# Summing the outputs of a bias network's second layer: one more addition by DMA, and half the third-layer matmuls

## The chip, the cores and the metric

The kernel runs on one core of a Trainium2 chip. The metric is the device time of one execution in microseconds (us). PE is the matmul engine, DVE the vector engine, ACT the scalar engine, POOL the GpSimd engine and SP the engine that issues most transfers. POOL issues the transfers that add to their destination, SP the plain ones.

## The reference

Four layers follow one another on a tensor of 2 x 512 x 32 x 32. The change is in the first, an attention whose keys are sampled at learned places. Cut to what matters (G = 8 groups, 64 keys, 1024 queries, two images):

```python
pos  = grid_q[:, :, None, :] - grid_kv[:, None, :, :]      # 16 x 1024 x 64 x 2
bias = sign(pos) * log1p(abs(pos))
bias = relu(bias @ cpb_w1 + cpb_b1)                        # 2 -> 128
bias = relu(bias @ cpb_w2 + cpb_b2)                        # 128 -> 128
bias = (bias @ cpb_w3 + cpb_b3).reshape(b, G, 1024, 64)    # 128 -> 1
sim  = einsum('bhid,bhjd->bhij', qh, kh) + bias
out  = einsum('bhij,bhjd->bhid', softmax(sim), vh)
x    = x + conv1x1(out)                                    # then an MLP, and three more layers
```

The bias network runs for each of 16 (image, group) and each of 64 keys on 1024 queries: a million positions with 128 features each. It takes most of the kernel's time.

## The kernel before

All is float32. `g` counts 8 steps: four chunks of 128 channels (two heads each) by two images. Within a step there are J = 64 keys; `n` counts all 512 keys, `p` their 256 pairs.

**First layer** (`first`, L351, DVE). The position feature of x depends on the column alone and that of y on the row alone, so the first layer is a table of columns plus a table of rows, with the relu folded into the same instruction. For one key it writes `h1`, 128 features x 2048 positions (32 rows, 2 heads, 32 columns). Four buffers of `h1` are all the lead that DVE can have over PE.

**Second layer** (`second`, L617, PE). The 128 outputs are taken in four sets `o` of 32. For a pair of keys and a set there are 8 matmuls of 32 outputs x 512 positions: four blocks of positions, each to its own 32 partitions of `ph`, for two keys. ACT applies bias and relu (L626) and leaves `r0` to `r3` in turn, each 128 partitions (4 blocks x 32 outputs) x 2 keys x 512. The weights have been scaled by the size of the third layer's weights, so what is left of the third layer is a sum with signs. The outputs were sorted at the start (`counted`, with the constants `same`, `below`, `place`, `rank`): among those that will be added to one another, sets 0 and 2 hold only the sign of the majority, and `rel` (plus or minus one) carries that of sets 1 and 3.

**Summing.** `combine` (L632, DVE) adds r1 to r0 and r3 to r2, with `rel`. `join` (L635, POOL's DMA) adds r2 to r0. Each block now has 32 sums per position and key. `shift` (L642, two DMAs of SP) copies, for the first key of the pair, one half of the partitions of r0 to the other half of a tile `xs`, and for the second key the reverse; `fold` (L647, two DMAs of POOL) adds the remaining partitions. One `xs` tile (128 x 512) thus holds one pair, 16 sums of each key.

**Third layer** (`third`, L656, PE). For 8 keys (four pairs), four matmuls of 32 rows, one per pair and each to its own 32 partitions of `psim`, sum each key's 16 partitions with their sign (`cw3`). Four such calls fill one `psim` tile of 32 keys: 8 calls for a step g, 64 in all.

**The order.** The engines' orders are fixed by the program: `pin` keeps them. The loop over pairs issues the second layer, and between sets runs what `at(n, when, ...)` has registered for key n. Registered are the attention of the step before (`attend`), the sampling and projection of the next step's keys and values (`prepare`, with `keys` on ACT, L725, and `values` on DVE, L737), the offset network of the later chunks (`Chain`, whose 36 taps, L229, run on DVE among the tables of keys 4 to 84 and 95 to 211), the table loads of SP and their scaling on ACT (L172), and the summing:

```python
for u in range(8):
    at(J * g + 8 * u + 14, 0, third, g, u)
...
at(2 * p + 4, 0, shift, p)
at(2 * p + 5, 0, fold, p)
```

`join` of a pair is issued during the next pair. The tile `co` holds the sample coordinates of all chunks. After the loop, `po` (L1035) applies the output weights to the attention's result; the scheduler mixes its matmuls with the last third-layer sets and the last step's softmax.

Of the kernel before, what the change touches and what calls it, by code (L numbers as in the profile page):

```python
# [10 lines left out]
F32 = mybir.dt.float32  # L11
AF = mybir.ActivationFunctionType
ALU = mybir.AluOpType
# [3 lines left out]
P = 128  # L17
B, C, H, W = 2, 512, 32, 32
HW = H * W
NT = B * HW  # L20
KC = C // P
TK = 8
DH = 64
J = 64
# [3 lines left out]
MID = C // 4  # L28
SE = C // 16
EPS = 1e-5  # L30
FMAX = float(np.finfo(np.float32).max)


# [21 lines left out]

_CONSTS = [("ident", P), ("grid", 2 * J), ("gridf", J), ("npx", 1), ("npy", 8), ("sel3", 2)]

_ORDER = [("same", P), ("below", P), ("place", P), ("rank", 1), ("third", 35)]
_CAT, _n = {}, 0
for _name, _w in _CONSTS:  # L60
    _CAT[_name] = (_n, _w)
# [10 lines left out]
def conv_seq(  # L72
# [20 lines left out]
    nc = tc.nc  # L93
# [6 lines left out]
    x = keep.tile([P, KC, NT], F32, name="x")  # L100
# [33 lines left out]
    with ExitStack() as ctx_l0:  # L134
        l0 = ctx_l0.enter_context(tc.tile_pool(name="l0", bufs=1))
# [2 lines left out]
        kblk = l0.tile([P, 2, 2, J], F32, name="kblk")  # L138
        vblk = l0.tile([P, 2, 2, J], F32, name="vblk")

        co = l0.tile([P, 2, 2, KC * B * J], F32, name="co")
        kvw = l0.tile([P, 2, KC, P], F32, name="kvw")
        wo = l0.tile([P, KC, C], F32, name="wo")
        ctx_att = ctx_l0.enter_context(ExitStack())
# [41 lines left out]
        def pin(ins):  # L186
            return tc.keep_in_program_order(ins) if started else ins
# [12 lines left out]
        class Chain:  # L200


            def __init__(self, k0, k1, alloc):
                self.k0, self.n, self.alloc = k0, (k1 - k0) * P, alloc
                self.g = slice(k0 * B, k1 * B)
                self.cs = slice(k0 * P, k1 * P)
                self.sums = {}

            def tile(self, name):
# [123 lines left out]

        w2a = l0.tile([P, 4, 32], F32, name="w2a")
        sb3 = l0.tile([P, 4, 2], F32, name="sb3")
        cw3 = l0.tile([P, 35], F32, name="cw3")
        rel = l0.tile([P, 2], F32, name="rel")

        h1p = ctx_att.enter_context(tc.tile_pool(name="h1p", bufs=4))
# [21 lines left out]
        with tc.tile_pool(name="a", bufs=1) as a, tc.tile_pool(name="aps", bufs=3, space=PSUM) as aps, tc.tile_pool(  # L363
            name="apc", bufs=1, space=PSUM
# [95 lines left out]
            def counted():  # L460
                pin(ve.tensor_copy(od[:, 7:9], pcnt))
                pin(ve.tensor_scalar(cpbw, cpbw, maj, None, ALU.mult))


                pin(ve.tensor_scalar(maj, total, 4.0, None, ALU.is_ge))
                pin(ve.tensor_scalar(t0, maj, -1.0, 1.0, ALU.mult, ALU.add))
                pin(ve.tensor_scalar(t1, total, -1.0, 8.0, ALU.mult, ALU.add))
# [127 lines left out]
        with tc.tile_pool(name="hid", bufs=3) as hid, tc.tile_pool(name="sm", bufs=1) as sm, tc.tile_pool(name="hps", bufs=2, space=PSUM) as hps, tc.tile_pool(  # L595
# [1 line left out]
        ) as sps, tc.tile_pool(name="mps", bufs=2, space=PSUM) as mps:  # L597
            NG, NK = KC * B, KC * B * J
            rs, psims = {}, {}
            todo = {}  # L600

            def at(n, when, fn, *args):

                todo.setdefault((n, when), []).append((fn, args))
# [5 lines left out]
            def second(p, o):  # L610

                ph = hps.tile([P, 2, 512], F32, name="ph")
                for i in range(2):
                    for t in range(4):
                        half, h = divmod(t, 2)
                        pin(
                            nc.tensor.matmul(  # L617
                                ph[t * 32 : (t + 1) * 32, i, :],
                                lhsT=w2a[:, o],
                                rhs=h1s[2 * p + i][:, half * 16 : (half + 1) * 16, h, :],  # L620
                                start=True,
                                stop=True,
                            )
                        )
                r = hid.tile([P, 2, 512], F32, name=f"r{o}", bufs=(4, 1, 3, 1)[o])
                pin(nc.scalar.activation(r, ph, AF.Relu, bias=sb3[:, o, 1:2]))  # L626
                rs[p, o] = r

# [5 lines left out]
            def join(p):  # L634
                pin(nc.gpsimd.dma_start(rs[p, 0], rs.pop((p, 2)), accum_op=ALU.add))  # L635

            def shift(p):

                r = rs[p, 0]
                xs = rs[p] = hid.tile([P, 512], F32, name="xs", bufs=5)  # L640
                for i in range(2):
                    pin(nc.sync.dma_start(xs[i::2], r[1 - i :: 2, i, :]))  # L642

            def fold(p):
                r = rs.pop((p, 0))
                for i in range(2):
                    pin(nc.gpsimd.dma_start(rs[p][i::2], r[i::2, i, :], accum_op=ALU.add))  # L647

            def third(g, u):
                kb, i = divmod(u, 4)  # L650
                p = (g * J + 8 * u) // 2
                if i == 0:
                    psims[g, kb] = sps.tile([P, 512], F32, name=f"psim{kb}")
                for m in range(4):
                    pin(
                        nc.tensor.matmul(  # L656
                            psims[g, kb][m * 32 : (m + 1) * 32, :],
                            lhsT=cw3[:, 3 - i : 35 - i],
                            rhs=rs.pop(p + m),
                            start=(i == 0),  # L660
                            stop=(i == 3),
                            skip_group_check=True,
                        )
                    )

            def prepare(g):

                k, b = divmod(g, B)
                st = {}
                n = J * (g - 1) + 30  # L670
                def hat(t):
                    if t == 0:
                        st["smp"] = smpp.tile([P, 8, 2, J], F32, name="smp")
                    pin(
                        nc.scalar.activation(
                            st["smp"][:, t],
                            co[:, 1, :, g * J : (g + 1) * J],
                            AF.Abs,
                            bias=c("npy")[:, t : t + 1],
                        )  # L680
                    )
# [4 lines left out]

                def cross(i):
                    sp = st["smp"][:, 4 * i : 4 * i + 4]
                    hx = co[:, 0, :, g * J : (g + 1) * J]
# [21 lines left out]
                def project():  # L711
                    st["pk"] = mps.tile([P, 2, J], F32, name="pk", tag="m")
                    for i in range(2):
# [3 lines left out]
                            )  # L717
                        )

                def keys():  # L720

                    for h in range(2):
                        hs = slice(h * DH, (h + 1) * DH)
                        pin(
                            nc.scalar.activation(  # L725
                                kblk[hs, g % 2, h, :].rearrange("p (k x i) -> p k x i", k=2, i=4),
                                st["pk"][hs, 0, :].rearrange("p (k i x) -> p k x i", k=2, i=4),
                                AF.Identity,
                                scale=DH**-0.5,
                            )  # L730
                        )

                def values():
                    for h in range(2):
                        hs = slice(h * DH, (h + 1) * DH)
                        pin(
                            nc.vector.tensor_copy(  # L737
                                vblk[hs, g % 2, h, :].rearrange("p (k x i) -> p k x i", k=2, i=4),
                                st["pk"][hs, 1, :].rearrange("p (k i x) -> p k x i", k=2, i=4),
                            )  # L740
                        )

                def weigh():
                    pw = st["pw"] = mps.tile([P, C], F32, name="pw", tag="m")
# [152 lines left out]
                    )  # L897
            for g in range(NG):
                prepare(g)
                for u in range(8):  # L900
                    at(J * g + 8 * u + 14, 0, third, g, u)
                if g < NG - 1:
                    attend(g, J * (g + 1) + 7, True)
            for p in range(NK // 2):
                at(2 * p + 4, 0, shift, p)
                at(2 * p + 5, 0, fold, p)

            def chain(k0, k1, n, taken):
                ch = Chain(k0, k1, lambda shape, name: mps.tile(shape, F32, name=name, tag="m"))
# [11 lines left out]
                for dn, when, fn, *args in plan:  # L921
                    at(n + dn, when, fn, *args)

            chain(1, 2, 84, 80)
            chain(2, 4, 211, 116)


            for k in range(KC):
# [951 lines left out]
def _layout(a):  # L1880
# [34 lines left out]
    def put(name, x, to=consts):  # L1915
        at, w = _CAT[name]
        to[:, at : at + w] = x
# [17 lines left out]
    put("place", np.array([0, 1, 4, 5, 2, 3, 6, 7])[rank].astype(f)[None], order)  # L1935
    put("rank", rank.astype(f)[:, None], order)
    put("third", (np.arange(35)[None] == (3 + 8 * (p // 32) + 4 * (p % 2))[:, None]).astype(f), order)
    put("npy", -(4 * np.arange(8)[None] + p[:, None] // 32).astype(f))


# [54 lines left out]
```

## Time and profile before

| | us |
|---|---|
| median of three runs | 2724.9 (2724.87 to 2726.49) |
| the profiled execution, its own time | 2726.49 |
| its span | 2724.7 |
| PE busy | 2681.3 |
| DVE busy | 2253.8 |
| ACT busy | 1538.4 |
| POOL busy | 670.2 |

A row of a group gives line, engine, operation, output <- inputs, shape and count; then busy time and mean ns of one; then the idle time of the engine just before these instructions and what ended most of it. One float32 matmul leaves two records. Matmuls on different column blocks run beside one another, so a row's mean of one is not its share of the time; the time from one set's start to the next one's is. The issues of DMAs give a median time from issue to landing: 4.8 us for `join` (512 KB), 4.7 for each DMA of `fold` and 2.2 for each of `shift` (128 KB each).

### The profile page before, as it was taken

Reading aid. Unit: us, or ns where it says so; the run is one execution under the profiler, and the core shown is the slowest. Engines: PE = TensorE matmul, PEld = TensorE weight load, DVE = VectorE, ACT = ScalarE, POOL = GpSimd, SP = SyncE. Lnnn points to the kernel's source line nnn. Section 1 sums busy time; section 2 is a strip of 40 time slices with the busy share of each in tenths; the row PEclk is TensorE's granted clock in tenths of the full one; section 3 lists DMA queues with packets and bytes.
Section 4 is the critical chain, followed back from the end, with each engine's and each line's share of the span. In section 5 each row is a group of like instructions: output and inputs, shape, how many; then the busy total and the mean of one; then the engine's idle time right before and its main releaser. Section 6 shows DMA issues by size and latency. Waiting matters only on the chain.

```text
span 2724.7 us, 49360 instructions
## 1 busy us (share of the span) xinstructions
PE 2681.3 (98%) x19830; PEld 978.1 (36%) x19830; DVE 2253.8 (83%) x1993; ACT 1538.4 (56%) x1904; POOL 670.2 (25%) x784
## 2 busy tenths in 40 slices
PE   8999999999999999999999999999999999999997
PEld 4223323232332323333333233333344444455544
DVE  6999999999999999999999999999554544615646
ACT  7676687667668766866766776776221111001334
POOL 0333333333333333333333333333100000000001
PEclk9999999999999999999999999999999999999998
DMA  3777777877777787777787788787410000100001
GB/s 128 165 167 164 161 157 156 172 154 161 168 155 160 155 174 155 161 167 157 168 193 164 157 174 189 156 172 157 94 30 23 16 23 24 39 38 1 0 0 62
DMA packets 146196, 335.13 MB, mean 123 GB/s; under 512 B 22672, under 2 KB 32400, under 8 KB 145200
## 3 DMA queue, kind: packets, MB, share of 16 engines
q0 software_dynamic: 77824, 201.38, 41.5%
q1 hardware_dynamic: 67568, 130.08, 13.6%
q8 instruction: 157, 2.57, 0.4%
q14 instruction: 71, 0.58, 0.1%
q10 hardware_dynamic: 576, 0.51, 0.1%
HBM read 58.99 MB, written 4.46 MB: 23 GB/s over the span
## 4 chain that ended last, share of the span: by engine, by line
PE 89%; DVE 6%; issue 3%; ACT 2%; DMA 0%; DVEq 0%; POOL 0%; ACTq 0%; POOLq 0%
PE ph L617 58%; PE A L1100 4%; PE D L1100 4%; PE C L1100 4%; PE B L1100 2%; PE psim L656 2%; PE po L1035 2%; DVE h L351 2%; DVE r L632 2%; PE pg L1243 1%; PE pa L1354 1%; PE pu L1277 1%; PE pscore L1486 1%; PE pz L1515 1%; PE pt L1506 1%
## 5 line engine op out<-in xcount | busy, mean ns | idle before, releaser
L617 PE MATMUL ph<-h,w2a 128*32 128x512 f32 x16384 | 1781.7, 592 | 4.3 <-ACT r L626 3.6
L626 ACT ACTIVATE r<-ph,sb 128x1024 f32<-128x1024 f32 x1024 | 1141.6, 1115 | 533.2 <-PE ph L617 508.1
L351 DVE CUSTOM_DVE_ANT_1 h<-tab 128x2048 f32<-128x2048 f32 x512 | 1171.1, 2287 | 22.4 <-PE ph L617 17.7
L617 PEld LDWEIGHTS ph<-h,w2a 128*32 128x32 f32 x16384 | 522.2, 109 | 1219.8 <-issue 832.0
L632 DVE SCALAR_TENSOR_TENSOR r<-r,rel,r 128x1024 f32<-128x1024 f32 x512 | 656.2, 1282 | 26.8 <-ACT r L626 26.5
L647 POOL DMA_DIRECT2D xs<-r x512 | 475.0, 1128 | 225.7 <-DMA xs<-r 122.7
L635 POOL DMA_DIRECT2D r<-r x256 | 222.6, 869 | 1047.8 <-DVE r L632 874.5
L172 ACT ACTIVATE tab<-tab,vec 128x256 f32<-128x256 f32 x252 | 137.1, 544 | 0.0
L1288 POOL MEMSET M<- 128x512 f32 x2 | 1.0, 518 | 443.8 <-DVE x L1164 443.8
L1140 ACT COPY u<-A 128x512 f32<-128x512 f32 x16 | 9.4, 586 | 146.9 <-PE A L1100 146.9
L1771 POOL TENSOR_TENSOR x<-x,aff 128x512 f32<-128x512 f32 x7 | 7.0, 1029 | 329.1 <-ACT e L1736 329.1
L1119 ACT ACTIVATE h<-h,vec 128x512 f32<-128x512 f32 x32 | 23.1, 721 | 113.6 <-DVE h L1122 113.6
L656 PE MATMUL psim<-xs,cw 128*32 128x512 f32 x512 | 70.5, 594 | 2.2 <-DMA xs<-r 2.2
L1122 DVE TENSOR_TENSOR h<-C,u 128x512 f32<-128x512 f32 x32 | 22.1, 691 | 47.7 <-PE C L1100 47.4
L1100 PE MATMUL A<-xn,w 128*128 128x512 f32 x128 | 60.3, 593 | 0.8 <-DVE x L1042 0.8
L1100 PE MATMUL C<-hT,w 128*128 128x512 f32 x128 | 60.3, 592 | 0.0
L1100 PE MATMUL A<-h,w 128*128 128x512 f32 x128 | 60.1, 592 | 0.0
L1035 PE MATMUL po<-q,vwo 128*128 128x512 f32 x128 | 57.1, 599 | 0.0
L229 DVE SCALAR_TENSOR_TENSOR acc<-q,vec,acc 128x128 f32<-128x128 f32 (+3 forms) x88 | 45.9, 521 | 0.8
L1160 DVE TENSOR_TENSOR x<-D,x 128x512 f32<-128x512 f32 x32 | 22.1, 691 | 26.0 <-PE D L1100 26.0
L852 ACT ACTIVATE e<-e,den 128x64 f32<-128x64 f32 x128 | 41.8, 337 | 2.2 <-DVE den L848 2.2
L1160 DVE TENSOR_TENSOR x<-C,x 128x512 f32<-128x512 f32 x32 | 22.1, 691 | 24.8 <-PE C L1100 24.8
(364 smaller groups left out, 1840.3 us busy)
## 6 DMA issues: line engine op xcount, KB each, us to landing
r<-r POOLq DMA_DIRECT2D x256, 512.0 KB, 4.8
xs<-r SPq DMA_DIRECT2D x512, 128.0 KB, 2.2
xs<-r POOLq DMA_DIRECT2D x512, 128.0 KB, 4.7
tab<-fd SPq DMA_DIRECT2D x63, 512.0 KB, 6.2
lw<-in_l_w_dram SPq DMA_DIRECT2D x5, 1024.0 KB, 9.1
x<-in_x_dram SPq DMA_DIRECT2D x4, 1024.0 KB, 9.0
w<-in_mlp_w_dram SPq DMA_DIRECT2D x8, 512.0 KB, 4.4
w<-in_mlp_w_dram SPq DMA_DIRECT2D x16, 256.0 KB, 3.2
```

Source lines behind the costliest of these rows:

```text
L172: return nc.scalar.activation(tf, tf if src is None else src[:, :, ax, :], AF.Identity, bias=0.0 if ax == 0 else v("L0_conv_cpb_b1"), scal ...
L229: pin(nc.vector.scalar_tensor_tensor(dst, src, wt_, dst, ALU.mult, ALU.add))
L351: nc.vector._custom_dve(TENSOR_ADD_SAT, out=h1, in0=columns.unsqueeze(1).to_broadcast([P, 32, 2, 32]), in1=rows_.unsqueeze(3).to_broadcast ...
L617: nc.tensor.matmul(ph[t * 32 : (t + 1) * 32, i, :], lhsT=w2a[:, o], rhs=h1s[2 * p + i][:, half * 16 : (half + 1) * 16, h, :], start=True, ...
L626: pin(nc.scalar.activation(r, ph, AF.Relu, bias=sb3[:, o, 1:2]))
L632: pin(nc.vector.scalar_tensor_tensor(r0, r1, rel[:, i : i + 1], r0, ALU.mult, ALU.add))
L635: pin(nc.gpsimd.dma_start(rs[p, 0], rs.pop((p, 2)), accum_op=ALU.add))
L647: pin(nc.gpsimd.dma_start(rs[p][i::2], r[i::2, i, :], accum_op=ALU.add))
L656: nc.tensor.matmul(psims[g, kb][m * 32 : (m + 1) * 32, :], lhsT=cw3[:, 3 - i : 35 - i], rhs=rs.pop(p + m), start=(i == 0), stop=(i == 3), ...
L1035: nc.tensor.matmul(po, lhsT=vwo[:, k * B + t // 2, o * P : (o + 1) * P], rhs=q[:, k, ts_], start=(k == 0), stop=(k == KC - 1),)
L1100: nc.tensor.matmul(banks[bank], lhsT=a[an][k], rhs=b_[bn_][k], start=(i < 4 and k == 0), stop=(k == n - 1), skip_group_check=True,)
L1160: nc.vector.tensor_tensor(to, t, to, ALU.add)
```

## The change

For one pair, the summing goes one step further before the third layer. `fold` now adds in place, in r0 itself, every odd partition to the even one before it, both keys in one DMA. `shift` copies every fourth partition of r0 to partitions d, d+4, ... of `xs`, and `meet` adds to them the partitions two further on. An `xs` tile (now 128 x 2 x 512, three buffers instead of five of half the size) takes d = 0 to 3, four pairs; each key has 8 sums. The third layer runs on two `xs` tiles at a time, 16 keys in four matmuls: four calls for a step g, 32 in all. The order of outputs at the start is over sets of 16 instead of 8, `r0` has five buffers instead of four, `co` keeps three chunks instead of four (the third chunk takes the first one's place), and `keys` and `values` write their new key order in four small copies each instead of two. The dates in the list move to fit.

```diff
+CO_AT = (1, 0, 1, 2)
...
-        co = l0.tile([P, 2, 2, KC * B * J], F32, name="co")
+        co = l0.tile([P, 2, 2, 3 * B * J], F32, name="co")
...
-                pin(ve.tensor_scalar(maj, total, 4.0, None, ALU.is_ge))
+                pin(ve.tensor_scalar(maj, total, 8.0, None, ALU.is_ge))
...
-                r = hid.tile([P, 2, 512], F32, name=f"r{o}", bufs=(4, 1, 3, 1)[o])
+                r = hid.tile([P, 2, 512], F32, name=f"r{o}", bufs=(5, 1, 3, 1)[o])
...
+            def fold(p):
+                r = rs[p, 0]
+                pin(nc.gpsimd.dma_start(r[0::2], r[1::2], accum_op=ALU.add))
+
             def shift(p):
-                r = rs[p, 0]
-                xs = rs[p] = hid.tile([P, 512], F32, name="xs", bufs=5)
-                for i in range(2):
-                    pin(nc.sync.dma_start(xs[i::2], r[1 - i :: 2, i, :]))
-
-            def fold(p):
-                r = rs.pop((p, 0))
-                for i in range(2):
-                    pin(nc.gpsimd.dma_start(rs[p][i::2], r[i::2, i, :], accum_op=ALU.add))
+                t, d = divmod(p, 4)
+                if d == 0:
+                    xs_[t] = hid.tile([P, 2, 512], F32, name="xs", bufs=3)
+                pin(nc.sync.dma_start(xs_[t][d::4], rs[p, 0][0::4]))
+
+            def meet(p):
+                t, d = divmod(p, 4)
+                pin(nc.gpsimd.dma_start(xs_[t][d::4], rs.pop((p, 0))[2::4], accum_op=ALU.add))
 
             def third(g, u):
-                kb, i = divmod(u, 4)
-                p = (g * J + 8 * u) // 2
+                kb, i = divmod(u, 2)
                 if i == 0:
                     psims[g, kb] = sps.tile([P, 512], F32, name=f"psim{kb}")
-                for m in range(4):
-                    pin(
-                        nc.tensor.matmul(
-                            psims[g, kb][m * 32 : (m + 1) * 32, :],
-                            lhsT=cw3[:, 3 - i : 35 - i],
-                            rhs=rs.pop(p + m),
-                            start=(i == 0),
-                            stop=(i == 3),
-                            skip_group_check=True,
+                for a in range(2):
+                    xs = xs_.pop(g * J // 8 + 2 * u + a)
+                    for c in range(2):
+                        m = 2 * c + a
+                        pin(
+                            nc.tensor.matmul(
+                                psims[g, kb][m * 32 : (m + 1) * 32, :],
+                                lhsT=cw3[:, 1 - i : 33 - i],
+                                rhs=xs[:, c, :],
+                                start=(i == 0),
+                                stop=(i == 1),
+                                skip_group_check=True,
+                            )
                         )
-                    )
...
-                    for h in range(2):
-                        hs = slice(h * DH, (h + 1) * DH)
...
+                    for h, kb in np.ndindex(2, 2):
+                        hs, ks = slice(h * DH, (h + 1) * DH), slice(kb * 32, (kb + 1) * 32)
+                        to, of = ordered(kblk[hs, g % 2, h, ks], st["pk"][hs, 0, ks])
+                        pin(nc.scalar.activation(to, of, AF.Identity, scale=DH**-0.5))
...
-                for u in range(8):
-                    at(J * g + 8 * u + 14, 0, third, g, u)
+                for u in range(4):
+                    at(J * g + 16 * u + 24, 0, third, g, u)
                 if g < NG - 1:
-                    attend(g, J * (g + 1) + 7, True)
+                    attend(g, J * (g + 1) + 9, True)
             for p in range(NK // 2):
-                at(2 * p + 4, 0, shift, p)
-                at(2 * p + 5, 0, fold, p)
+                at(2 * p + 4, 0, fold, p)
+                at(2 * p + 6, 0, shift, p)
+                at(2 * p + 7, 0, meet, p)
...
-            chain(1, 2, 84, 80)
-            chain(2, 4, 211, 116)
+            chain(1, 2, 86, 82)
+            chain(2, 4, 213, 116)
...
-    rank = p // 32 * 2 + p % 2
-    same = p[:, None] % 32 // 2 == p[None] % 32 // 2
+    rank = p // 32 * 4 + p % 4
+    same = p[:, None] % 32 // 4 == p[None] % 32 // 4
```

More of the change, by code (lines that the diff above doesn't have):

```diff
@@ L56 @@
 _CONSTS = [("ident", P), ("grid", 2 * J), ("gridf", J), ("npx", 1), ("npy", 8), ("sel3", 2)]
-_ORDER = [("same", P), ("below", P), ("place", P), ("rank", 1), ("third", 35)]
+_ORDER = [("same", P), ("below", P), ("place", P), ("rank", 1), ("third", 33)]
 _CAT, _n = {}, 0
@@ L205, in __init__ @@
                 self.g = slice(k0 * B, k1 * B)
-                self.cs = slice(k0 * P, k1 * P)
+                self.cs = slice(CO_AT[k0] * P, (CO_AT[k0] + k1 - k0) * P)
                 self.sums = {}
@@ L337, in conv_seq @@
         sb3 = l0.tile([P, 4, 2], F32, name="sb3")
-        cw3 = l0.tile([P, 35], F32, name="cw3")
+        cw3 = l0.tile([P, 33], F32, name="cw3")
         rel = l0.tile([P, 2], F32, name="rel")
@@ L462, in counted @@
                 pin(ve.tensor_scalar(cpbw, cpbw, maj, None, ALU.mult))
-                pin(ve.tensor_scalar(maj, total, 4.0, None, ALU.is_ge))
+                pin(ve.tensor_scalar(maj, total, 8.0, None, ALU.is_ge))
                 pin(ve.tensor_scalar(t0, maj, -1.0, 1.0, ALU.mult, ALU.add))
-                pin(ve.tensor_scalar(t1, total, -1.0, 8.0, ALU.mult, ALU.add))
+                pin(ve.tensor_scalar(t1, total, -1.0, 16.0, ALU.mult, ALU.add))
                 pin(ve.scalar_tensor_tensor(t0, t1, t0, below, ALU.mult, ALU.add))
@@ L599, in conv_seq @@
             rs, psims = {}, {}
-            todo = {}
+            xs_, todo = {}, {}
             def at(n, when, fn, *args):
@@ L669, in prepare @@
                 st = {}
-                n = J * (g - 1) + 30
+                n = J * (g - 1) + 32
+                here = slice(CO_AT[k] * P + b * J, CO_AT[k] * P + (b + 1) * J)
                 def hat(t):
@@ L676, in hat @@
                             st["smp"][:, t],
-                            co[:, 1, :, g * J : (g + 1) * J],
+                            co[:, 1, :, here],
                             AF.Abs,
@@ L688, in cross @@
                     sp = st["smp"][:, 4 * i : 4 * i + 4]
-                    hx = co[:, 0, :, g * J : (g + 1) * J]
+                    hx = co[:, 0, :, here]
                     pin(nc.vector.tensor_tensor(sp, sp, hx.unsqueeze(1).to_broadcast([P, 4, 2, J]), ALU.mult))
@@ L718, in project, with ordered @@
                         )
+                def ordered(to, of):
+                    to, of = to.rearrange("p (c x i) -> p c x i", c=2, i=2), of.rearrange("p (i x c) -> p c x i", c=2, i=2)
+                    return to, of
                 def keys():
-                    for h in range(2):
-                        hs = slice(h * DH, (h + 1) * DH)
[L724 to L731, printed above, removed]
-                def values():
[L734 to L741, printed above, removed]
+                    for h, kb in np.ndindex(2, 2):
+                        hs, ks = slice(h * DH, (h + 1) * DH), slice(kb * 32, (kb + 1) * 32)
+                        to, of = ordered(kblk[hs, g % 2, h, ks], st["pk"][hs, 0, ks])
+                        pin(nc.scalar.activation(to, of, AF.Identity, scale=DH**-0.5))
+                def values():
+                    for h, kb in np.ndindex(2, 2):
+                        hs, ks = slice(h * DH, (h + 1) * DH), slice(kb * 32, (kb + 1) * 32)
+                        to, of = ordered(vblk[hs, g % 2, h, ks], st["pk"][hs, 1, ks])
+                        pin(nc.vector.tensor_copy(to, of))
                 def weigh():
@@ L1929, in _layout @@
     put("sel3", (p[:, None] % 32 == np.array([1, 2])[None]).astype(f))
-    rank = p // 32 * 2 + p % 2
-    same = p[:, None] % 32 // 2 == p[None] % 32 // 2
+    rank = p // 32 * 4 + p % 4
+    same = p[:, None] % 32 // 4 == p[None] % 32 // 4
     put("same", same.astype(f), order)
     put("below", (same & (rank[:, None] < rank[None])).astype(f), order)
-    put("place", np.array([0, 1, 4, 5, 2, 3, 6, 7])[rank].astype(f)[None], order)
+    put("place", (np.array([0, 2, 1, 3])[p // 32] * 4 + p % 4).astype(f)[None], order)
     put("rank", rank.astype(f)[:, None], order)
-    put("third", (np.arange(35)[None] == (3 + 8 * (p // 32) + 4 * (p % 2))[:, None]).astype(f), order)
+    put("third", (np.arange(33)[None] == (1 + 8 * (p // 32) + 2 * (p % 4))[:, None]).astype(f), order)
     put("npy", -(4 * np.arange(8)[None] + p[:, None] // 32).astype(f))
```

## The prediction

> **What bounds the kernel now.** First the page: busy time by engine, then the costliest groups.
>
> ```profile
> PE 2681.3 (98%) x19830; PEld 978.1 (36%) x19830; DVE 2253.8 (83%) x1993; ACT 1538.4 (56%) x1904; POOL 670.2 (25%) x784
> ...
> L617 PE MATMUL ph<-h,w2a 128*32 128x512 f32 x16384 | 1781.7, 592 | 4.3 <-ACT r L626 3.6
> ...
> L351 DVE CUSTOM_DVE_ANT_1 h<-tab 128x2048 f32<-128x2048 f32 x512 | 1171.1, 2287 | 22.4 <-PE ph L617 17.7
> ...
> L632 DVE SCALAR_TENSOR_TENSOR r<-r,rel,r 128x1024 f32<-128x1024 f32 x512 | 656.2, 1282 | 26.8 <-ACT r L626 26.5
> L647 POOL DMA_DIRECT2D xs<-r x512 | 475.0, 1128 | 225.7 <-DMA xs<-r 122.7
> L635 POOL DMA_DIRECT2D r<-r x256 | 222.6, 869 | 1047.8 <-DVE r L632 874.5
> ...
> L656 PE MATMUL psim<-xs,cw 128*32 128x512 f32 x512 | 70.5, 594 | 2.2 <-DMA xs<-r 2.2
> ```
>
> PE is bound by the second layer (L617); the third (L656) is 512 records, two for each of 256 matmuls. But DVE is near the end of its time too, and a mean over the whole span hides it: the bias loop runs from 44 to 1924 us, 1880 us for 256 pairs of keys, 7.34 us a pair. So I ask for stretches of that loop.
>
> ```profile
> 100.00:200.00 100.00, 100.00 (x940) 30.10 (x936) 100.00 (x71) 72.41 (x80) 36.05 (x42) 1.00 0.78 168
> 200.00:300.00 100.00, 99.84 (x942) 30.30 (x938) 99.69 (x72) 68.48 (x73) 36.25 (x42) 1.00 0.76 163
> 300.00:600.00 300.00, 298.11 (x2761) 93.73 (x2757) 294.38 (x209) 216.18 (x256) 103.21 (x120) 1.00 0.75 159
> 600.00:900.00 300.00, 298.31 (x2750) 91.90 (x2743) 295.08 (x204) 219.89 (x276) 104.03 (x121) 1.00 0.75 162
> 900.00:1400.00 500.00, 499.46 (x4686) 156.06 (x4681) 480.55 (x300) 358.18 (x418) 176.58 (x206) 1.00 0.76 163
> 1400.00:1900.00 500.00, 500.00 (x4652) 155.28 (x4648) 481.81 (x298) 355.66 (x408) 177.61 (x208) 1.00 0.79 171
> ```
>
> After the length come PE, PEld, DVE, ACT and POOL busy, clock, DMA share, GB/s. PE is full throughout. DVE idles 0.3 us from 100 to 300 (offset taps L229 between its tables), 5.6 and 4.9 us in the next two stretches, 37.6 us after 900. The timelines give PE's price for a third-layer set and DVE's lead over PE:
>
> ```profile
> 1190.38 1.04 PE L656 MATMUL psim<-xs,cw 128*32 128x512 f32 x8
> 1191.24 1.04 PE L617 MATMUL ph<-h,w2a 128*32 128x512 f32 x8
> ...
> 601.38 2.28 DVE L351 CUSTOM_DVE_ANT_1 h<-tab 128x2048 f32<-128x2048 f32 x1
> ...
> 605.60 1.11 ACT L626 ACTIVATE r<-ph,sb 128x1024 f32<-128x1024 f32 x1 [0.60 <-PE ph L617]
> ```
>
> Four matmuls, one per column block, take 0.86 us start to start. A pair's four relus (L626) start 1.72 us apart, each 1.75 us after PE starts its half tables: PE began the pair at 605.60 at 603.85 and needed its second table at 604.71; DVE had finished that at 603.66. **Lead 1.05 us** at pair 76. The same reading gives 1.7 at pair 20, 1.4 at 40, 1.5 at 104, and 2.1 to 3.9 from 112 on.
>
> [...]
>
> **The change part by part.**
>
> 1. Third layer: 64 sets of four become 32. 32 x 0.86 = **-27.5 us** of PE. All on PE, which is full, so it counts wherever DVE can follow.
>
> 2. DVE early. DVE loses no work. Until pair 112 (872 us) the sets issued fall from 27 to 13, so PE would run 14 x 0.86 = 12.0 us ahead. DVE can give its lead plus idle it may drop. At pair 40: lead 1.4, idle since pair 12 about 1.8, against 4.3 asked: 3.2. At 76: 1.05 + 6.0 = 7.1, against 7.7. At 104: 1.5 + 7.6 = 9.1, against 11.2. Some of that idle is for relus behind table loads on ACT and stays; I take half of the 6 us at pair 76 as lasting. That leaves 4 at 76 and, by what PE saves or DVE idles until 112, 7 there: **+5.0** against 12.0. Ends: +2.5 (all idle goes) and +9 (lead only). After 112 DVE idles over 37 us for the 15.5 us asked: nothing lost; the page's h wait on ph (17.7 us) shrinks first.
>
> 3. keys and values: two copies of 64x64 per group become four of 64x32. L725 is 212 ns and L737 222 ns (groups); the smaller ones take at most that. ACT +16 x 0.21 = 3.4 us, hidden in its 28% idle. DVE +16 x 0.2 = 3.2; three of the eight groups fall where DVE is full: 6 x 0.2 = 1.2, **+1.0** taken (0 to 2.4, should vblk also wait for the longer kblk).
>
> 4. DMAs. Per pair: join 512 KB stays; fold is now 256 KB in place, shift 128 KB instead of 256, meet 128 KB. POOL still issues three (about 0.86 to 1.13 us each), SP one instead of two. Accumulated bytes go from 768 to 896 KB a pair, copied from 256 to 128. From 300 to 1800 us q0 is 60% and q1 16% of the engines; scaled by bytes (q1's 84 MB lose 27) 70 and 11: 81% of engine time instead of 76. No row has the in-place accumulate; nearest is L647, landing in 4.7 us; bounds 2.6 to 9.0. Priced at **0**, hidden by slack: meet of p is issued after join of p+2. With combine (DVE r) ending up to 5.5 us into the next pair, it lands some 10 us after pair p+3 starts; the third layer reads it at p+5, 4 us later, and r0 (five buffers) is rewritten 6 us later. PE queues everything behind L656, so without that cover its lateness is paid in full.
>
> 5. POOL's queue in the changed program: join k, meet k-2, fold k, join k+1. Fold k waits for join k (4.8 us, page's issues) and holds all behind it: 4.8 + 0.86 = 5.7 us, below PE's fastest pair of 4 x 1.72 = 6.9. Meet k-2 waits for SP's shift, whose fold went out a pair earlier, so it is ready. SP's table loads (6.2 us) stand between shifts as before, issued about ten keys early. **0**.
>
> 6. co's three slots, the later chain starts (+2 keys), constants, r0 and xs buffers: no added instruction, and their readers stay as far off as before. **0**.
>
> 7. End of the loop. Accumulates after the last relu become three deep: 4.8 + 4.7 + 2.2 + 4.7 = 16.4 us, about when the last set ran before (1941.6, 17 after the relu's end at 1924.5). Meanwhile PE in the changed program has one set, two flips and 19 po matmuls, some 17.7 us of its 18. Against 2.2 us idle now (L656): **0**, from -2 to +3.
>
> Sum: -27.5 + 5.0 + 1.0 = **-21.5 us**. The profiled run took 2726.5 (span 2724.7 and 1.8 around it): 2705.0. It was the slowest of three, 1.6 above the median 2724.9; against that, **2703.4**.
>
> **The rivals.**
>
> (a) DVE fully bound early: ACT's waits stay and copies cost more. Gain 15.5 after pair 112, 12.0 - 9 before, less 2.4: 16; down to 8 if the attention steps (drops of 1.7 us of lead a group) also stop PE later. 2709 to 2717. For: 100.00 of 100 above. Against: 37 us idle later.
>
> (b) PE keeps all: 2724.9 - 27.5 = 2697.4, or 2695 if the end's 2.2 us idle goes too. Against: lead of 1.05 at pair 76.
>
> (c) Slower: POOL's in-order hold. Fold k and join k+1 then overlap. 201 MB took 41.5% of 2724.7 us, so 178 GB/s for accumulates: fold's 256 KB add 1.5 us and meet's 128 KB 0.7 to a landing of 4.8. A turn is 7.0 + 0.86 = 7.8 us instead of 7.34: 256 x 0.5 = +120, about 2845. It decides from a join landing above 6.0 us. For: landings up to 9.2 in the trace. Against: the median, and that fold normally lands before the next join starts.
>
> (d) It doesn't shorten the path: sets of order 0, 2, 1, 3 overlap worse, 1.7 us a set, or DVE gives nothing early and later. About 2725.
>
> **How the numbers follow.** Main forecast 0.66 (2698 to 2709), (a) 0.15, (b) 0.08, (c) 0.07, (d) 0.04. A measurement of this kernel can tell about 0.2%, 5.4 us, from no change. Faster: 0.66 + 0.15 + 0.08 = 0.89; same 0.04; slower 0.07. The range runs over (a) and (b), 2695 to 2717, leaving (c) and (d) out.
>
> **What would show it.** Right: 256 psim records with the set still 0.86 us; DVE without idle until about 870 us and PE with new waits for h (L351) of some 5 us there; none later; PE's psim waits under 3 us in all; POOL's fold waiting for join's landing but join still waiting for DVE. Wrong: PE waiting on psim for DMA through the loop, ACT r waiting for meet, or join on POOL waiting for DMA rather than DVE; or a PE gap of several us at the last set.

## The result and the profile after

The median of the changed kernel is **2697.7 us** (2695.6 to 2698.0, four runs) beside 2725.1 for the kernel before: ratio 0.9897, 95% interval 0.988 to 0.9914. The forecast was 2703.4, in a range of 2695 to 2717. The profiled run took 2697.67; its span is 2695.9, against 2724.7 before: 28.8 us less. First the page: busy time by engine, then the costliest groups (busy us, mean ns of one, then idle before them and what ended it).

```profile
PE 2653.6 (98%) x19574; PEld 967.3 (36%) x19574; DVE 2251.3 (84%) x2009; ACT 1538.4 (57%) x1920; POOL 669.8 (25%) x784
...
L619 PE MATMUL ph<-h,w2a 128*32 128x512 f32 x16384 | 1779.1, 593 | 6.0 <-ACT r L628 3.3
...
L353 DVE CUSTOM_DVE_ANT_1 h<-tab 128x2048 f32<-128x2048 f32 x512 | 1172.9, 2291 | 13.0 <-PE ph L619 10.0
...
L634 DVE SCALAR_TENSOR_TENSOR r<-r,rel,r 128x1024 f32<-128x1024 f32 x512 | 658.0, 1285 | 16.4 <-ACT r L628 15.8
L642 POOL DMA_DIRECT2D r<-r x256 | 219.5, 857 | 961.2 <-DMA r<-r 936.1
L637 POOL DMA_DIRECT2D r<-r x256 | 245.2, 958 | 280.4 <-DVE r L634 243.6
L653 POOL DMA_DIRECT2D xs<-r x256 | 306.6, 1198 | 12.2 <-issue 6.1
```

PE has 256 instructions fewer, exactly the third layer's, and DVE and ACT each 16 more, the copies. The second layer (L619) costs what it did. On POOL three lines stand where two stood. Join (L637) waited 1048 us before, mostly for DVE; now fold (L642) waits 961 us for the transfer of join, and of join's own wait 280 us are left. So POOL's time of waiting moved to the instruction behind join, 3.75 us a pair, and from those 280 us I estimate that 1.1 us a pair remains before it turns into a delay. The list of DMA issues (count, KB each, median us from issue to landing) has the two that matter:

```profile
r<-r POOLq DMA_DIRECT2D x256, 512.0 KB, 5.2
r<-r POOLq DMA_DIRECT2D x256, 256.0 KB, 3.4
```

Join lands in 5.2 us (4.8 before), fold in place in 3.4. (Shift takes 3.9 us instead of 2.2, meet 5.6. PE waits for neither in the loop; relus wait 5.4 us in all for meet to free r0.) Now PE's timeline around one third-layer set in the middle of the loop: start, us, engine, line.

```profile
1185.48 1.04 PE L664 MATMUL psim<-xs,cw 128*32 128x512 f32 x8
1186.34 13.92 PE L619 MATMUL ph<-h,w2a 128*32 128x512 f32 x128
```

A set is still 0.86 us start to start, with eight records of 592 ns each (median of L664), so its four matmuls run beside one another as before. The stretches of the loop, in the columns of the forecast:

```profile
100.00:200.00 100.00, 99.74 (x927) 29.05 (x922) 100.00 (x70) 71.80 (x81) 36.45 (x43) 1.00 0.80 166
200.00:300.00 100.00, 99.54 (x936) 29.93 (x932) 99.92 (x74) 69.30 (x76) 34.64 (x41) 1.00 0.79 161
300.00:600.00 300.00, 297.98 (x2761) 93.22 (x2757) 298.62 (x215) 219.07 (x261) 105.40 (x123) 1.00 0.79 164
600.00:900.00 300.00, 297.31 (x2734) 90.82 (x2730) 297.87 (x207) 220.90 (x280) 105.28 (x123) 1.00 0.78 162
900.00:1400.00 500.00, 499.46 (x4680) 156.02 (x4676) 487.21 (x309) 363.94 (x428) 177.92 (x207) 1.00 0.79 167
1400.00:1900.00 500.00, 500.00 (x4652) 154.87 (x4646) 483.04 (x303) 359.26 (x414) 181.10 (x210) 1.00 0.81 171
```

DVE's idle time from 300 to 900 us fell from 10.5 to 3.5 us, and PE is no longer at 100.00 in the first stretch: DVE sets the pace there now. After 900 us DVE has 30 us idle and PE is full. To put the gain in its place I read when PE starts each pair of keys in both traces (start of its first relu, less 1.75 us):

| pair | 20 | 40 | 76 | 112 | 160 | 200 | 255 | end of the last ph | first A, L1100 / L1105 |
|---|---|---|---|---|---|---|---|---|---|
| after is ahead by, us | 1.3 | 2.4 | 6.3 | 8.0 | 12.6 | 16.8 | 21.9 | 22.8 | 28.7 |

Here ph is the second layer's output, and A (L1100 before, L1105 after) the first matmul of the next part of the kernel. Three pieces, then: **8.0 us until pair 112**, where the sets that are gone ask for 12.0; **14.8 after it**, of 15.5; and **5.9 behind the loop**, where the forecast had nothing. How DVE holds PE back is seen in the timeline before pair 76:

```profile
588.94 2.27 DVE L353 CUSTOM_DVE_ANT_1 h<-tab 128x2048 f32<-128x2048 f32 x1
...
591.27 0.23 PEld L619 LDWEIGHTS ph<-h,w2a 128*32 128x32 f32 x8 [0.62 <-DVE h L353]
```

DVE ends a table at 591.21, and the weight load of the first matmul on it goes at 591.27, after 0.62 us of idle time. By the same reading as in the forecast the lead at pair 76 is 0.45 us where it was 1.05. The wait stands at the weight load. The page counts as many of these as of matmul records (19574 of each), and the load comes first: at L664 the first one starts at 131.2 us, the first matmul at 131.6. The list of waits from 44 to 870 us (total us, times, longest) has for the weight loads, after:

```profile
PEld ph L619 <- DVE h L353: 30.4, 45, 1.3
```

and before:

```profile
PEld ph L617 <- DVE h L351: 8.9, 13, 1.2
```

These waits are not lost time one for one: PE's matmuls run without a gap for 12.22 us from 587.05 on while that weight load waits, and 21.5 us more of such waits go with 4 us less gain. The piece behind the loop is in PE's timeline there. Before:

```profile
1923.12 1.02 PE L656 MATMUL psim<-xs,cw 128*32 128x512 f32 x2
...
1926.29 1.80 PE L656 MATMUL psim<-xs,cw 128*32 128x512 f32 x2 [2.15 <-DMA xs<-r]
1928.51 7.68 PE L1035 MATMUL po<-q,vwo 128*128 128x512 f32 x16
1936.12 1.05 PE L656 MATMUL psim<-xs,cw 128*32 128x512 f32 x2
1937.09 4.56 PE L1035 MATMUL po<-q,vwo 128*128 128x512 f32 x10
1941.58 1.05 PE L656 MATMUL psim<-xs,cw 128*32 128x512 f32 x2
```

After:

```profile
1900.35 1.03 PE L664 MATMUL psim<-xs,cw 128*32 128x512 f32 x4
...
1901.77 16.57 PE L1040 MATMUL po<-q,vwo 128*128 128x512 f32 x38
1918.27 1.05 PE L664 MATMUL psim<-xs,cw 128*32 128x512 f32 x4
```

A matmul leaves two records here. Before, the last set of four ran as four single matmuls with po between them, each taking alone (1936.12 to 1937.09: 0.97 us) no less than a full set of four, and one of them idled 2.15 us for its transfer and then took 1.80. Afterwards the same set runs as two pairs of 1.0 us and waits for nothing. That is 4.9 + 2.15 - 2.1 = 5.0 us; the po matmuls (L1035, then L1040) take 0.8 less in all.

### The profile page after: what moved, and what is told of

Same layout as the page of the kernel before. It is cut to its first block, busy times and chain, and to the rows that moved or that the text cites. A ratio compares the mean times of both kernels' runs of the same rounds, so it can differ in the third digit from the quotient of the medians.

```text
span 2695.9 us, 48423 instructions
## 1 busy us (share of the span) xinstructions
PE 2653.6 (98%) x19574; PEld 967.3 (36%) x19574; DVE 2251.3 (84%) x2009; ACT 1538.4 (57%) x1920; POOL 669.8 (25%) x784
## 4 chain that ended last, share of the span: by engine, by line
PE 81%; DVE 9%; issue 6%; ACT 2%; DMA 1%; POOL 1%; DVEq 0%; ACTq 0%; POOLq 0%
PE ph L619 51%; DVE h L353 4%; PE A L1105 4%; PE D L1105 4%; PE C L1105 4%; DVE r L634 3%; PE B L1105 2%; PE po L1040 2%; PE pg L1248 1%; PE pa L1359 1%; PE pu L1282 1%; PE psim L664 1%; PE pscore L1491 1%; DMA xs<-r 1%; PE pt L1511 1%
## 5 line engine op out<-in xcount | busy, mean ns | idle before, releaser
L619 PE MATMUL ph<-h,w2a 128*32 128x512 f32 x16384 | 1779.1, 593 | 6.0 <-ACT r L628 3.3
L619 PEld LDWEIGHTS ph<-h,w2a 128*32 128x32 f32 x16384 | 520.2, 109 | 1226.6 <-issue 801.7
L642 POOL DMA_DIRECT2D r<-r x256 | 219.5, 857 | 961.2 <-DMA r<-r 936.1
L637 POOL DMA_DIRECT2D r<-r x256 | 245.2, 958 | 280.4 <-DVE r L634 243.6
L653 POOL DMA_DIRECT2D xs<-r x256 | 306.6, 1198 | 12.2 <-issue 6.1
L1105 PE MATMUL A<-xn,w 128*128 128x512 f32 x128 | 60.3, 593 | 0.8 <-DVE x L1047 0.8
L1105 PE MATMUL C<-hT,w 128*128 128x512 f32 x128 | 60.3, 592 | 0.0
L1105 PE MATMUL A<-h,w 128*128 128x512 f32 x128 | 60.1, 592 | 0.0
L1040 PE MATMUL po<-q,vwo 128*128 128x512 f32 x128 | 56.3, 594 | 0.0
## 6 DMA issues: line engine op xcount, KB each, us to landing
x<-in_x_dram SPq DMA_DIRECT2D x4, 1024.0 KB, 10.5
```

The source lines that it names most:

```text
L619: nc.tensor.matmul(ph[t * 32 : (t + 1) * 32, i, :], lhsT=w2a[:, o], rhs=h1s[2 * p + i][:, half * 16 : (half + 1) * 16, h, :], start=True, ...
L642: pin(nc.gpsimd.dma_start(r[0::2], r[1::2], accum_op=ALU.add))
L653: pin(nc.gpsimd.dma_start(xs_[t][d::4], rs.pop((p, 0))[2::4], accum_op=ALU.add))
L1040: nc.tensor.matmul(po, lhsT=vwo[:, k * B + t // 2, o * P : (o + 1) * P], rhs=q[:, k, ts_], start=(k == 0), stop=(k == KC - 1),)
L1105: nc.tensor.matmul(banks[bank], lhsT=a[an][k], rhs=b_[bn_][k], start=(i < 4 and k == 0), stop=(k == n - 1), skip_group_check=True,)
```

## The experiments

Theory A: the gain is 0.86 us for each set that is gone, less what DVE holds back until pair 112, and beside it a separate gain at the end of the loop. The main doubt was whether POOL's hold (fold waiting for join) costs something that a better order would give back, or nearly does so. Each ratio below is to the kernel before, run beside it.

**e1_before_whole_end** takes the end of the loop alone: the kernel before, with its last set turned round, so that the tile that lands last is asked for first and the four matmuls stay together.

```diff
-                for m in range(4):
+                for m in (range(3, -1, -1) if (g, u) == (NG - 1, 7) else range(4)):
```

> The kernel before; only the last third-layer call issues its four matmuls in reverse order, so the one that waits longest stands first and the four run as one set. Theory A (of the 28.8 us that the span fell, 22.8 came in the bias loop and 5.8 at its end, where the kernel before splits its last set into four single matmuls of 0.98 us among the po matmuls and idles 2.2 us): the singles cost 3.9 us, one set 0.9, but PE has only 13 po matmuls to fill the wait, so it idles some 3 to 4 us: 2723.0, between 2721 and 2725. Theory B (the end is no cost of its own, all 28.8 us are the 32 sets of the loop): 2724.9, no change within 0.5.

Measured: 2722.1 beside 2725.6, ratio 0.9987 (0.9981 to 0.9994). Pair 255 starts 0.4 us later than before, and A 3.4 us earlier, so 3.8 us are won behind the loop. (The span fell by 5.4, from 2724.7 to 2719.3, but 2.0 of that lie behind A, where nothing was changed; that part takes from 731.3 to 733.3 us in the traces of all runs.) PE's timeline shows the set in one piece:

```profile
1937.30 1.33 PE L656 MATMUL psim<-xs,cw 128*32 128x512 f32 x8 [0.94 <-DMA xs<-r]
```

The split set was a cost of its own, which had nothing to do with the number of sets. It accounts for 3.8 of the 5.9 us behind the loop; most of the other 2.1 are two waits that PE still has here and not after the change: 0.94 us for this transfer and 0.87 for a relu ahead of po.

**e2_after_64_sets** keeps everything of the change except the saving: the first half of each accumulation is issued three times, so that PE runs 64 sets again. The same values are written again each time, so the output stays.

```diff
-                for a in range(2):
-                    xs = xs_.pop(g * J // 8 + 2 * u + a)
+                pair = [xs_.pop(g * J // 8 + 2 * u + a) for a in range(2)]
+                for a in [0, 1] * (1 if i else 3):
+                    xs = pair[a]
```

> The changed kernel with the first matmuls of every psim tile issued three times (the same values are written again): 64 sets of four on PE again instead of 32, all else as changed. Theory A: the loop's gain of 22.8 us goes, the end's 5.8 stays: 2697.7 + 22.8 = 2720.5, between 2718 and 2722, and in the trace PE starts pair 255 within 2 us of the kernel before. Theory B: all of the gain goes, 2725, between 2723 and 2727. If the order of the DMAs had brought part of the gain by itself: below 2716.

Measured: 2721.7, ratio to before 0.9984 (0.9978 to 0.9991). PE's timeline at the end of the loop:

```profile
1914.72 10.05 PE L619 MATMUL ph<-h,w2a 128*32 128x512 f32 x92
1924.59 1.03 PE L665 MATMUL psim<-xs,cw 128*32 128x512 f32 x4
```

The last ph ends at 1924.77, 1.5 us later than before and 24.2 later than after; up to there 63 sets have run here and before. The gain behind the loop stays (5.9 us from that point to A). So the longer chain of DMAs, the in-place fold, the moved steps and the copies together cost the loop 1.5 us where PE has its old length: 0.8 of it by pair 112, where both have run 27 sets, and 0.7 after. All that the loop gains is the missing sets.

**e3_after_whole_end** turns the last set of the changed kernel round in the same way.

```diff
-                for a in range(2):
+                for a in (1, 0) if (g, u) == (NG - 1, 3) else (0, 1):
```

> The changed kernel; the last third-layer call takes its two xs tiles in reverse order, so its four matmuls run together at the end instead of two and two. Theory A: 1.0 us less of PE (two halves of 0.98 become one set of 0.98), less up to 0.9 of new idle before the last data land: 2697.2, between 2696.5 and 2698. Theory B: no change, 2697.7.

Measured: 2696.4, ratio 0.9896 (0.988 to 0.9911). The set is whole and starts without idle time, but PE idles 0.87 us for a relu just before po. The median is 1.3 below after, inside both intervals, and in the trace A starts 0.3 us later than in after: nothing is won at the end of the loop.

**e4_after_few_taps and e5_before_few_taps** lighten DVE by leaving out 30 of the 36 offset taps of each of the two later chains, in both kernels. The offsets, and so the output, are then others.

```diff
+                    if tap[1] != 1:
+                        continue
```

> The changed kernel with 30 of the 36 taps of both later offset chains left out (the offsets of chunks 1 to 3 are then others), which takes about 60 x 0.6 us = 36 us from DVE while keys 4 to 213 run. Theory A (DVE's full time before pair 112 costs PE 4.0 of the 12.0 us that fewer sets free there): PE keeps them, 2697.7 - 4.0 = 2693.7, between 2692.5 and 2695, and the gain at pair 112 against the kernel before with the same cut is about 12. Theory B (DVE held nothing back): 2697.7, within 1.

> The kernel before with the same 30 taps of 36 left out of both later chains (other offsets for chunks 1 to 3). Theory A: PE was full there and hardly waited for DVE: 2724.9, at most 1.5 us less. If the cut itself speeds PE up (fewer DVE accesses beside it): 3 us or more below.

Measured: 2691.8 (ratio 0.9874, 0.986 to 0.9889) and 2723.6 (0.9994, 0.9985 to 1.0002). With DVE lightened in both, the change is 12.05 us ahead at pair 112, where the missing sets ask for 12.0; with the full DVE it was 8.0. **DVE's lack of lead costs 4.0 us**, the copies that stand on DVE included. The same stretch of the loop in e4:

```profile
600.00:900.00 300.00, 299.23 (x2766) 92.89 (x2762) 291.72 (x193) 225.19 (x284) 106.27 (x125) 1.00 0.79 163
```

DVE idles 8.3 us there instead of 2.1, and PE has 299.23 instead of 297.31. e4 came out 0.7 us below its interval; the kernel before gains 1.5 us from the missing taps too, the most that had been allowed for it. After pair 112 the gain is again 14.8 of 15.5 us, so the missing 0.7 do not come from DVE's taps.

**e6_after_fold_late** puts fold behind the next join in POOL's queue, where join's transfer has landed by then, so that nothing is held.

```diff
-                at(2 * p + 4, 0, fold, p)
+                at(2 * p + 4, 1, fold, p)
```

> The changed kernel with fold registered half a step later, so that POOL issues fold of a pair after join of the next pair instead of ahead of it. In the changed kernel fold waits 961 us in all for join's landing and holds POOL. Theory C (this hold is hidden; a turn of POOL has 1.1 us of slack a pair): within 1.5 us of 2697.7, with fold's waits for the DMA under 150 us. Theory D (the hold costs something): faster by 3 us or more. Slower by 3 us or more if shift and meet, now half a pair later, come late for the third layer.

Measured: 2703.6, ratio 0.9921 (0.9908 to 0.9935), 6 us slower than after. Of fold's wait for the transfer only 24 us are left, and join waits for DVE as it did before. Up to pair 184 PE stays within 0.5 us of after, but for single pairs: no time was to be had from the hold. What is lost is lost in two places, at pairs 185 (2.7 us) and 217 to 219 (6.2 us), where SP's four 1 MB loads of x are issued: shift and meet come later (around the later pair of loads meet waits 7.0 us for shift, until 1623.6, and then 6.0 until 1642.8), and a relu waits for meet to free its r0 buffer.

```profile
ACT r L628 <- DMA xs<-r: 11.6, 6, 4.1
```

(ACT's waits from 44 to 1900 us; in after the sum is 5.4 us and no single wait over 0.6.) Neither theory had this time; the third branch of the expectation, 3 us or more lost to a late chain, is what came true.

**e7_after_fold_two and e8_after_fold_three** make fold's issue longer, as more DMAs of the same bytes: two of 64 partitions, and one of 64 with two of 32.

```diff
-                pin(nc.gpsimd.dma_start(r[0::2], r[1::2], accum_op=ALU.add))
+                for lo, hi in ((0, 64), (64, 128)):
+                    pin(nc.gpsimd.dma_start(r[lo:hi:2], r[lo + 1 : hi : 2], accum_op=ALU.add))
```

(e8 has the bounds 0, 64, 96, 128.)

> The changed kernel with fold in two DMAs of 32 partitions (the same rows and bytes). POOL's turn is join's landing plus fold's issues: 5.2 + 2 x 0.86 = 6.9 us, still below the mean pair of 7.25. Theory C (POOL binds only when its turn passes the pair): within 3 us of 2697.7. Theory D (POOL is at its limit already): each added issue is paid in full, 256 x 0.86 = +220 us, or a good part of it.

> The changed kernel with fold in three DMAs of 32, 16 and 16 partitions (the same rows and bytes). POOL's turn: 5.2 + 3 x 0.86 = 7.8 us, above the mean pair of 7.25. Theory C: POOL becomes the bound, 256 x 0.53 = +136 us: 2834, between 2790 and 2880, with PE waiting for DMAs at psim or ACT at r. If the bytes and not the issues set the pace: within 5 us of 2697.7.

Measured: 2898.5 (ratio 1.0637, 1.062 to 1.0655) and 2859.4 (1.0492, 1.046 to 1.0524). By its number e7 is what theory D had said (201 of 220 us), but D should make e8 dearer still, and two issues cost more than three. e8 fell into the interval of theory C, which e7 had missed by 200 us. No one theory fits both. The DMA view of e7, 300 to 1800 us (queue, packets, MB, share of 16 engines; then issues):

```profile
q0 software_dynamic: 53568, 170.70, 72.3%
...
r<-r POOLq DMA_DIRECT2D x186, 512.0 KB, 6.7
r<-r POOLq DMA_DIRECT2D x373, 128.0 KB, 4.4
```

In 1500 us only 186 joins went out, 8.06 us a pair instead of 7.25; join lands in 6.7 us instead of 5.2, and relus wait for meet:

```profile
ACT r L628 <- DMA xs<-r: 198.4, 109, 6.3
```

Queue q0 needs 0.723 x 1500 / 186 = 5.83 us of all engines for a pair, against 4.89 in after (67.5%, 207 joins); in e8 it is 5.75, with join landing in 5.7 us.

**e10_after_fold_late_two** joins e6 and e7: if the hold together with the second issue is the cause, moving fold behind the next join should cure it.

> The changed kernel with fold in two DMAs (as in e7, 2898 us) but issued after the next pair's join (as in e6, 2704 us): the same four issues a pair on POOL as in e7, but no hold of POOL for join's landing. Theory C2 (e7's 200 us come from fold k and join k+1 going out together, so that join lands in 6.7 us instead of 5.2 and POOL, held for it, turns in 6.7 + 0.86 + the second issue = 8 us): without the hold 2700 to 2715. Theory D (four issues a pair, or smaller DMAs, are too many in themselves): 2850 or more.

Measured: 2799.2, ratio 1.0277 (1.0253 to 1.0301), between both expectations. The hold did not go but moved. POOL's waits from 300 to 1800 us, for meet (xs) and for fold (r):

```profile
POOL xs L654 <- DMA xs<-r: 548.9, 92, 8.4
...
POOL r L643 <- DMA r<-r: 71.9, 53, 4.2
```

Meet waits 549 us for SP's shift to land, fold only 72, and q0 still takes 5.64 us a pair. So neither the hold nor its place is the whole of it; the transfers themselves had become dearer.

**e12_after_fold_two_wide** tells the two apart. It has the rows, bytes and number of issues of e7, but each DMA spreads its 32 rows over all 128 partitions.

```diff
-                pin(nc.gpsimd.dma_start(r[0::2], r[1::2], accum_op=ALU.add))
+                for i in (0, 2):
+                    pin(nc.gpsimd.dma_start(r[i::4], r[i + 1 :: 4], accum_op=ALU.add))
```

> The changed kernel with fold in two DMAs, as in e7 (same rows, bytes, issues and order on POOL), but the first takes every second of the 64 rows and the second the others, so that each reaches over all 128 partitions; in e7 each stayed within 64. Theory E (e7's loss comes mostly from slower transfers within half of the partitions: q0 takes 5.8 us of all 16 engines a pair there against 4.9 in the changed kernel, for the same bytes): q0 back to about 5.0 us a pair, join's landing near 5.3, POOL's turn 5.3 + 1.7 = 7.0: 2698 to 2720. Theory D2 (the fourth issue and the hold are enough by themselves): 2850 to 2900.

Measured: **2698.5**, ratio 0.9901 (0.9884 to 0.9919): after's time. The DMA view and ACT's waits, 300 to 1800 us:

```profile
q0 software_dynamic: 59469, 189.51, 69.2%
...
r<-r POOLq DMA_DIRECT2D x206, 512.0 KB, 5.2
r<-r POOLq DMA_DIRECT2D x413, 128.0 KB, 2.9
```

```profile
ACT r L628 <- DMA xs<-r: 2.0, 2, 1.2
```

q0 takes 5.04 us a pair. Both runs have 288 packets a pair in q0; the mean packet took 324 ns in e7 (72.3% of 16 engines over 1500 us, by 53568) and 279 in e12. The two kernels differ in nothing but the rows, so **e7's 200 us come from transfers that stay within half of the partitions**. A fourth issue on POOL costs nothing that shows, but it takes most of what POOL had to spare: join's waits for DVE from 300 to 1800 us, in after and in e12, are

```profile
POOL r L637 <- DVE r L634: 151.2, 109, 4.1
```

```profile
POOL r L637 <- DVE r L634: 20.2, 33, 1.4
```

e8 has no such counterpart. Its transfers are nearly as dear as e7's, but whether its five issues would be too many with all partitions reached is not shown.

**e9_after_values_act** takes e3 and puts the four copies of values (183 ns each) on ACT instead of DVE.

```diff
-                        pin(nc.vector.tensor_copy(to, of))
+                        pin(nc.scalar.copy(to, of))
```

> The changed kernel with the last third-layer set whole (as in e3) and the four copies of values on ACT instead of DVE: 32 x 0.185 = 5.9 us leave DVE, 2.2 us of them (three groups) before pair 112, where DVE is full. Theory A (before pair 112 PE gets back what DVE is spared): 2 us less than e3, about 1.3 + 2 = 3.3 us below the changed kernel, between 2 and 4. If ACT's added 0.7 us a group holds up the relus: no better than e3.

Measured: 2697.0, ratio 0.9894 (0.9878 to 0.9911), 0.6 above e3. In the trace PE starts pair 255 0.7 us earlier than in e3 where 2 were expected, and its weight loads still wait 24.1 us for h until 870 us. Theory A's size missed. The other branch, no better than e3, fits the time, but not by its reason: PE's matmuls wait no longer for ACT than in after (2.8 us until 870 us). Only the first of the three groups that fall before pair 112 gave something (0.9 us from pair 11 to 19, against e3); why the other two gave nothing stays open.

**e11_after_again** is the changed kernel itself, beside e10 and e12.

> The changed kernel itself, for a direct comparison with e9 and e10 on this chip: 2697.7, ratio to the kernel before 0.990.

Measured: 2698.0 (2697.7 to 2698.0), ratio 0.9899 (0.9884 to 0.9914). No variant with the same output beats the changed kernel by more than the intervals allow.

## Why the prediction was right

The mechanism of the loop was right, and the total came within 5.7 us; most of the difference is one term that had been put at zero, the end of the loop.

- **Step 1, -27.5, held.** A set still takes 0.86 us in the trace of after, and e2 with its 64 sets ends its last ph 24.2 us later than after, which takes back all of the 22.8 us gained there.
- **Steps 2 and 3, +5.0 and +1.0, measured together 4.0** (e4 against e5). The way of reading it was right: DVE's lead and half of its idle time were what PE could take. Somewhat more of the idle went than half: from 300 to 900 us 7.0 of the 10.5 us. The forecast's count at pair 76 is one set short: in the traces ten are gone there (8.6 us, not 7.7), of which 6.3 arrived. The copies were placed on the path at 1.0; e9 leaves 0.7 for those on DVE. The mark by which it was to be seen, new waits of PE for h, was there but elsewhere: PE's matmuls wait 2.1 us for h, not some 5, and the wait appears at the weight loads (30.4 us). After pair 112 the loop gained 14.8 of 15.5, where the forecast lost nothing. The 0.7 us are missing in e2 too, with all 64 sets, and in e4 against e5; so they belong to the other parts of the change, and which of them is open.
- **Step 4, 0, held.** Engine share rose to 0.78 to 0.81 (81% was said), q0 67.5% and q1 11.5%, 79.0 together (70 and 11). PE never waits for a transfer at psim through the loop; the in-place accumulate lands in 3.4 us, in the lower part of its bounds of 2.6 to 9.0.
- **Step 5, 0, held, with less to spare than was said.** Join lands in 5.2 us, not 4.8, so the hold is 5.2 + 0.86 = 6.1 us of a turn of 7.25. From 300 to 1800 us 109 of 207 joins still waited for DVE (151 us in all). e6 removes the hold and gains nothing in the 184 pairs before its own loss; e12 adds an issue behind the hold and loses nothing, but there only 33 joins still waited for DVE, for 20 us.
- **Step 7, 0, was mis-sized.** It measured 5.9 us, a gain beyond its -2 to +3. What could be won was priced by the 2.2 us of idle time alone. I read the group of L656, whose idle is 2.2, but not how its last set ran: as four single matmuls of no less than a set's length each. A group's mean over 512 records hides this; the timeline of the last 20 us would have shown it. e1 shows it as a cost of its own: 3.8 us come back when the set runs whole, though PE still waits twice. The reading of the changed program's own end held: its last set waits for nothing.
- **Rival (b)**, 2697.4 or 2695, is closer in time than the main forecast, but by luck: PE does not keep all (4.0 us go to DVE), and the end gives more than its 2.2 us; the two errors nearly cancel.
- **Rival (c)**, about 2845 us, did not come in the changed kernel, but e7 shows that it was a cliff nearby: join landing in 6.7 us, above the 6.0 from which it was to decide, a turn of 8.06 us where it had 7.8, and 200 us. What leads there in e7 is not the count of issues on POOL but where the rows of a transfer lie (e12, with as many issues, took 2698.5 us).

## What to carry to other kernels

A saving on a full engine was worth its time here only as far as the engine that feeds it had lead and idle time to give, stretch by stretch (8.0 of 12.0 us until pair 112, 14.8 of 15.5 after it); read the lead at several points of the loop and count what each stretch asks for. Look at the timeline of the last few instructions of a loop before pricing its end: matmuls meant to run side by side lost that where waits for single transfers split them up (the last set before: 0.97 us for one matmul, where four together take 0.86 in the loop). Where an accumulating DMA has to be split, split its rows as in e12, so that each part still reaches all partitions: 2698.5 us, against 2898.5 with each part within half of them (e7).

## What the hardware showed that was not expected

- The same 64 rows, added in place in two DMAs of 32 rows: within half of the partitions each (e7) 4.4 us to land and 5.83 us of all engines a pair for the whole queue; spread over all 128 partitions (e12) 2.9 us and 5.04 us. The 512 KB join beside them lands in 6.7 us in e7 and in 5.2 in e12. Why the rows matter is not shown.
- One matmul with 32 output columns between full-width ones takes 0.97 us (before, 1936.12 to 1937.09), no less than a set of four in the loop (0.86).
- Here moving a hold did not remove it: with fold behind the next join, meet waits for shift instead, 268 us in e6 and 549 in e10 from 300 to 1800 us, against 1.4 in after.
